# Moving gathered rows in 32-partition blocks and transposing them on VectorE in a top-2 expert layer

## Chip, cores and metric

The kernel runs on one core of a Trainium2 chip, in float32 throughout. The metric is device microseconds of one execution, as the median of several runs. Before the change the three runs gave 1540.99, 1541.81 and 1544.17 us, so the median is 1541.81 us.

## What is computed

The reference is a Mamba-2 block with a gated MLP, followed by a mixture of experts with eight experts of which each token takes two. `x` has 2048 rows (tokens) of 512 numbers.

```python
x = x + _L0_attn_ref(_layernorm(x), ...)      # Mamba-2 block and gated MLP
x = x + _L0_ffn_ref(_layernorm(x), Wr, Wg, Wu, Wd)

def _L0_ffn_ref(x, Wr, Wg, Wu, Wd):            # H=512, I=352, E=8, K=2
    probs = softmax(x @ Wr)                     # router, 8 columns
    topk_w, topk_idx = top_k(probs, 2); topk_w = topk_w / sum(topk_w)
    h = silu(x @ Wg[e]) * (x @ Wu[e])           # for the experts e of each token
    out = sum over the two e of  topk_w * (h @ Wd[e])
```

The change touches only the last part: how the rows of the normalised `x` get to the expert matmuls.

## The kernel before

**Stages.** Eight blocks of 256 tokens go through the Mamba part (`mamba`, `chunk`). From the third block on, the MLP of 512 tokens that are ready (`feed_forward`) is woven between them. The last MLP (tokens 1536 to 2047) runs alone. Then come the experts. The MLP leaves its result in DRAM (`out`), and the layer-normalised rows in `xnd` (all tokens) and `xnd1` (the first 1536): `route`, L586 to L673, writes them with `normed` (L594), transposes them for the router (`transposed`, L197), takes the two best experts per token, and scatters entries of token number and weight into per-expert lists in DRAM (L669, four indirect DMAs for each of two choices, issued by GpSimd).

**Tiles of the expert stage.** `table` (L932) turns the lists into tiles of 128 rows that all belong to one expert: ten from the first 1536 tokens (`NS1`, index `idx1`), 26 more once all tokens are routed (`idx2`). So 36 tiles (`NSA`) are always worked through, s = 0 to 35; three more stand behind a branch (L1123) that is taken only where they are filled. The weights of all eight experts lie in SBUF (`ew`).

**One tile** is this chain:

1. `gather(s)`, L1023: GpSimd issues an indirect DMA, 128 rows of 512 numbers from DRAM to `xg`, two buffers.
2. `front(s)`, L1031: four TensorE transposes of 128x128 into one PSUM bank (L201), and one ScalarE copy to SBUF (L203), which gives `xgT`: the 512 numbers of a row now lie on partitions.
3. `hidden(s)`, L1036: gate and up matmuls with `xgT` stationary (L1045, four steps of k, each for gate and up), in two halves with a pause between; SiLU on ScalarE (L1049), product on VectorE (L1050) gives `eh`.
4. `turned(s)`, L1053: three TensorE transposes of `eh`, copied out by VectorE (L1059, two thirds) and ScalarE (L1060, the last third) to `ehT`.
5. `back(s)`, L1063: three down matmuls (L1066; the last one reads ScalarE's third), scaling by the row's weight on VectorE (L1071), and an indirect DMA by GpSimd that adds the rows into `out` (L1072).

**Order.** TensorE's instructions stand as the program emits them (`manual_schedule`). For each tile s of `tiles()` (L1089) they are: transposes of tile s+1, first half of `hidden(s)`, transposes `turned(s-1)`, second half of `hidden(s)`, `back(s-1)`. The instructions of the other engines are put in order by a planner of the framework, which also inserts the waits. Each engine works its own queue strictly in order, and so a waiting instruction holds what stands behind it; a DMA issue stands in the queue of the engine that issues it. While tiles 0 to 4 run, the routing of the last 512 tokens is woven in (`second()`, L1112), and the second table comes out of it during tile 7.

**Buffers that matter.** `pmlp` has three buffers under the tag "mg", used by the MLP's weights (`mg`, `ms`, L526 and L539). `wk` has four under the tag "a" (the MLP's `a`, then `xgT` and `ehT`). `AHEAD = 2` (L1077) lets gathers be emitted two tiles ahead.

```python
    def transposed(src, dst, weight=None, kind="tr"):
        pt = bank(kind, [NK, P], "pt")
        for k in range(NK):
            nc.tensor.transpose(pt[:, k, :], src[:, k * P : (k + 1) * P], ident)
        if weight is None:
            nc.scalar.copy(dst, pt)
```

Of the kernel before, what the change touches and what calls it, by code (L numbers as in the profile page):

```python
# [9 lines left out]
F32 = mybir.dt.float32  # L10
I32 = mybir.dt.int32
AF = mybir.ActivationFunctionType
ALU = mybir.AluOpType
# [3 lines left out]
P = 128  # L17
T = 2048
D = 512
NK = D // P  # L20
# [12 lines left out]
FC = 128  # L33
NFC = DFF // FC
NE = 8
EI = 352
ET = [(0, 128), (128, 128), (256, 96)]


NS = (2 * T + NE * (P - 1)) // P  # L40

NS1 = 10


NSA = (2 * T + NE * (P // 2)) // P
EW = NK * 2 * EI + len(ET) * D
EPS = 1e-5
# [7 lines left out]
def mamba_mlp_moe(ctx, tc, x, w_in, w_out, w_gu, w_down, par, wr, wg, wu, wd, out):  # L55
# [3 lines left out]
    nc = tc.nc  # L59
# [13 lines left out]
    pmlp = ctx.enter_context(tc.tile_pool(name="pmlp", bufs=2, side="right"))  # L73
# [13 lines left out]
    w_o = pw.tile([P, 8, D], F32, name="w_o")  # L87
    wr_sb = const.tile([P, NK, NE], F32, name="wr_sb")

# [6 lines left out]
    def load_w_in(pair):  # L96
# [15 lines left out]
        out=tri, in_=ones, pattern=[[1, P]], compare_op=ALU.is_ge, fill=0.0, base=0, channel_multiplier=-1  # L112
# [3 lines left out]
        out=late, in_=ones, pattern=[[-1, P]], compare_op=ALU.is_gt, fill=0.0, base=0, channel_multiplier=1  # L116
# [3 lines left out]
    nc.gpsimd.memset(eps, EPS)  # L120
    rank = const.tile([P, NE], F32, name="rank")
    nc.gpsimd.iota(rank, pattern=[[-1, NE]], base=NE, channel_multiplier=0, allow_small_or_imprecise_dtypes=True)
    halo = pw.tile([P, 12, 3], F32, name="halo")
# [7 lines left out]
    upto = const.tile([P, NE, NE], F32, name="upto")  # L131
    nc.gpsimd.affine_select(
        out=upto, in_=ones[:, : NE * NE].rearrange("p (e f) -> p e f", e=NE), pattern=[[1, NE], [-1, NE]],
# [63 lines left out]
# [7 lines that stand above are left out]
        else:  # L204
            nc.vector.tensor_tensor(dst, pt, bc(weight, 2, P), ALU.mult)
# [121 lines left out]
    def finish(steps):  # L327
        while True:
            try:
                next(steps)  # L330
            except StopIteration as end:
                return end.value
# [187 lines left out]
    KH = NK // 2  # L520
# [65 lines left out]
    def route(fb, rows):  # L586

        mv2, rs2 = small("mv2", NJ, 2), small("rs2", NJ)
        for j in range(NJ):
            stats(small_p, rows[j], mv2[:, j, :])  # L590
        rsqrt_eps(rs2, mv2[:, :, 1])
        lg, l2, tmp = (small(n, NJ, NE) for n in ("lg", "l2", "tmp"))

        def normed(j):  # L594
            t = fb * NJ + j
            nc.scalar.dma_start(out=out[t * P : (t + 1) * P, :], in_=rows[j])
            xn = mid([D], f"xn{t}")
            nc.vector.tensor_scalar(xn, rows[j], mv2[:, j, 0:1], rs2[:, j : j + 1], ALU.subtract, ALU.mult)
            nc.scalar.dma_start(out=xnd[t * P : (t + 1) * P, :], in_=xn)
            if fb < NFB - 1:  # L600
                nc.scalar.dma_start(out=xnd1[t * P : (t + 1) * P, :], in_=xn)
            return xn

        def logits(j, xT):
            pl = bank("d", [NE], f"pl{fb}_{j}")
            for k in range(NK):
                nc.tensor.matmul(pl, xT[:, k, :], wr_sb[:, k, :], start=(k == 0), stop=(k == NK - 1))
            nc.vector.tensor_copy(lg[:, j, :], pl)

        xn = normed(0)  # L610
        yield
        for j in range(NJ):
            if j:
                logits(j - 1, xT)
            xT = mid([NK, P], f"xT{fb}_{j}")
            transposed(xn, xT)
            if j < NJ - 1:
                xn = normed(j + 1)
            yield
        logits(NJ - 1, xT)  # L620

        chosen = [small(n, NJ, NE) for n in ("o1", "o2")]
        m1, m2, *mr = (small(n, NJ) for n in ("rm1", "rm2", "mr1", "mr2"))

        def top(src, mx, mr, oh):

            nc.vector.tensor_reduce(mx, src, AX.X, ALU.max)
            nc.vector.tensor_tensor(tmp, src, bc(mx, 2, NE), ALU.is_equal)
            nc.vector.tensor_tensor(tmp, tmp, bc(rank, 1, NJ), ALU.mult)
            nc.vector.tensor_reduce(mr, tmp, AX.X, ALU.max)  # L630
            nc.vector.tensor_tensor(oh, tmp, bc(mr, 2, NE), ALU.is_equal)

        top(lg, m1, mr[0], chosen[0])
        nc.vector.scalar_tensor_tensor(l2, chosen[0], -3.0e38, lg, ALU.mult, ALU.add)
        top(l2, m2, mr[1], chosen[1])

        wt = [small(n, NJ) for n in ("wt1", "wt2")]
        nc.vector.tensor_tensor(m2, m2, m1, ALU.subtract)
        nc.scalar.activation(m2, m2, AF.Exp)
        nc.vector.tensor_scalar_add(wt[0], m2, 1.0)  # L640
        nc.vector.reciprocal(wt[0], wt[0])
        nc.vector.tensor_tensor(wt[1], m2, wt[0], ALU.mult)


        both, prior = small("both", NJ, NE), small("prior", NJ, NE)
        nc.vector.tensor_tensor(both, *chosen, ALU.add)
        nc.vector.tensor_copy(prior[:, 0, :], before)
        for j in range(1, NJ):
            nc.vector.tensor_tensor(prior[:, j, :], prior[:, j - 1, :], both[:, j - 1, :], ALU.add)
        nc.vector.tensor_tensor(before, prior[:, NJ - 1, :], both[:, NJ - 1, :], ALU.add)  # L650
        yield
        yield
        pr = bank("tr", [NJ, NE], f"pr{fb}")
        nc.tensor.matmul(pr, tri, both, start=True, stop=False)
        nc.tensor.matmul(pr, ones, prior, start=False, stop=True)
        nc.vector.tensor_copy(prior, pr)

        for n in range(2):

            at, to = small("at", NJ), small_p.tile([P, NJ], I32, name=f"to{n}", tag=f"to{n}")  # L660
            nc.vector.tensor_tensor(tmp, chosen[n], prior, ALU.mult)
            nc.vector.tensor_reduce(at, tmp, AX.X, ALU.add)
            nc.vector.scalar_tensor_tensor(at, mr[n], -float(T), at, ALU.mult, ALU.add)
            nc.vector.tensor_scalar_add(at, at, NE * T - 1.0)
            nc.vector.tensor_copy(to, at)
            entry = entries[:, n, fb * NJ : (fb + 1) * NJ, :]
            nc.vector.tensor_copy(entry[:, :, 1], wt[n])
            for j in range(NJ):
                nc.gpsimd.indirect_dma_start(  # L669
                    out=writers.pop(), out_offset=bass.IndirectOffsetOnAxis(ap=to[:, j : j + 1], axis=0),  # L670
                    in_=entry[:, j, :], in_offset=None,
                )
            yield  # L673
# [215 lines left out]
    for b in range(NB):  # L889
        fb, at = divmod(b, BPF)  # L890
# [132 lines left out]
    def gather(s):  # L1023
        n, (_, _, idx, _), src = of(s)
        xg = row(f"xg{s}")
        nc.gpsimd.indirect_dma_start(  # L1026
            out=xg, out_offset=None, in_=src, in_offset=bass.IndirectOffsetOnAxis(ap=idx[:, n : n + 1], axis=0)
        )
        return xg

    def front(s, xg):  # L1031
        xT = wk.tile([P, NK, P], F32, name=f"xgT{s}", tag="a", bufs=4)
        transposed(xg, xT)
        return xT

    def hidden(s, xT):  # L1036
        n, (exp_i, _, _, _), _ = of(s)
        e = nc.tensor.value_load(exp_i[0:1, n : n + 1], min_val=0, max_val=NE - 1)
        w = ew[:, bass.DynSlice(e, 1), :].rearrange("p a n -> p (a n)")
        pg = bank("g", [EI], f"epg{s}")  # L1040
        pu = bank("u", [EI], f"epu{s}")
        for k in range(NK):
            for a, ps in enumerate((pg, pu)):
                lo = (2 * k + a) * EI
                nc.tensor.matmul(ps, xT[:, k, :], w[:, lo : lo + EI], start=(k == 0), stop=(k == NK - 1))  # L1045
            if k == 1:
                yield
        h = mid([EI], f"eh{s}")
        nc.scalar.activation(h, pg, AF.Silu)  # L1049
        nc.vector.tensor_tensor(h, h, pu, ALU.mult)  # L1050
        return h, w
# [22 lines left out]
            compute_op=ALU.add,  # L1074
        )

    AHEAD = 2  # L1077
    rest = None
    got, xT = {}, {}

    def fetch(upto):

        for s in range(min(upto + AHEAD, NSA if rest else NS1)):
            if s not in got:
                got[s] = gather(s)
        if upto in got:
            xT[upto] = front(upto, got[upto])

    def tiles():  # L1089

# [32 lines left out]
    filled = nc.values_load(rest[0][0:1, NS - NS1 :], min_val=0, max_val=NS)  # L1123
    with tc.If(filled > NSA - NS1):
        for s in range(NSA, NS):
            h, w = finish(hidden(s, front(s, gather(s))))
            back(s, turned(s, h), w)


# [64 lines left out]
```

## Time and profile before

The profiled execution took 1540.27 us; its span from first to last instruction is 1538.6 us. Its granted TensorE clock is 0.994 of full speed.

| engine | busy us | share of span |
|---|---|---|
| TensorE matmuls (PE) | 1498.3 | 97% |
| TensorE weight loads (PEld) | 1021.0 | 66% |
| VectorE (DVE) | 749.8 | 49% |
| ScalarE (ACT) | 744.0 | 48% |
| GpSimd (POOL) | 425.5 | 28% |

The expert stage alone runs from about 1228 us to the end. In the stretch from 1300 to 1345 us the starts of one matmul group in successive tiles (the down matmuls at 1310.06, 1318.14, 1326.22, 1334.31) are 8.08 us apart: that is the period of one tile. From 1296 to 1400 us PE is busy in all of the 104.0 us, DVE in 22.1, ACT in 17.0 and POOL in 34.5; the DMA engines have a mean share of 0.40 there.

How to read a line of groups: source line, engine, operation, tile written and tiles read, size, and count; then busy time and the mean of one; then idle time of that engine just before, with what ended it. A busy PE isn't PE at its peak, since matmuls overlap: the pitch, from start to start, says more than the duration.

### The profile page before, as it was taken

The page shows a single profiled execution, that of the slowest core. Times are in us where ns is not written, and L with a number is a line of the kernel's source. Part 1 is how long each engine was busy: PE and PEld are TensorE (multiplying, and loading weights), DVE is VectorE, ACT ScalarE, POOL GpSimd, SP SyncE. Part 2 cuts the span into 40 slices and gives each one's busy share as a digit, 9 for nine tenths or more (in the row PEclk, how much of TensorE's full clock was granted, in tenths as well). Part 3 has the DMA queues.
Part 4 walks back from the last instruction along what each step waited for, and adds up shares of the span by engine and source line. Part 5 has one row for each costly group of instructions (what it writes and reads, how often), then busy time and mean ns, then how long its engine had stood idle before and what let it go on. Part 6 is the DMA issues. An engine that isn't in the chain of part 4 may idle for free. (4 is left out here: it accounts for less than half of the span.)

```text
span 1538.6 us, 18825 instructions
## 1 busy us (share of the span) xinstructions
PE 1498.3 (97%) x6153; PEld 1021.0 (66%) x6153; DVE 749.8 (49%) x1939; ACT 744.0 (48%) x1332; POOL 425.5 (28%) x537
## 2 busy tenths in 40 slices
PE   8899999999999999999999999999999999999996
PEld 7566577677667676767676677666776666566553
DVE  7776775645645564556454643334343433222221
ACT  5888967635663598458745754222221231111110
POOL 4432324424242212141212120411131124233321
PEclk9999999999999999999999999999999999999999
DMA  9444445545544554454335532426879434333332
GB/s 305 137 138 125 137 140 183 190 149 171 171 151 148 185 165 131 137 118 157 121 123 179 167 121 89 93 93 209 289 205 260 152 91 64 66 69 65 66 63 35
DMA packets 128241, 217.54 MB, mean 141 GB/s; under 512 B 12560, under 2 KB 72848, under 8 KB 128144
## 3 DMA queue, kind: packets, MB, share of 16 engines
q1 hardware_dynamic: 105376, 166.34, 35.6%
q0 software_dynamic: 9088, 18.91, 7.2%
q10 hardware_dynamic: 13680, 31.07, 5.4%
q8 instruction: 52, 0.85, 0.2%
q14 instruction: 45, 0.37, 0.1%
HBM read 175.48 MB, written 40.80 MB: 141 GB/s over the span
## 5 line engine op out<-in xcount | busy, mean ns | idle before, releaser
L691 PE MATMUL pd<-md,a 128*128 128x512 f32 x512 | 238.8, 593 | 0.8 <-DVE r L692 0.7
L340 PE MATMUL pm<-hT,wi 128*128 128x256 f32 x768 | 185.4, 386 | 3.7 <-DMA wi<-in_w_in 3.7
L340 PEld LDWEIGHTS pm<-hT,wi 128*128 128x128 f32 x768 | 141.7, 192 | 29.2 <-issue 7.9
L692 DVE TENSOR_TENSOR r<-r,pd 128x512 f32<-128x512 f32 x128 | 87.4, 684 | 150.6 <-PE pd L691 149.9
L691 PEld LDWEIGHTS pd<-md,a 128*128 128x128 f32 x512 | 96.9, 190 | 76.6 <-issue 65.8
L361 DVE SCALAR_TENSOR_TENSOR ca<-pre,params,ca 128x256 f32<-128x256 f32 x288 | 143.9, 557 | 0.3
L707 PE MATMUL py<-h2T,ms 128*128 128x256 f32 x512 | 131.7, 380 | 3.5 <-DMA ms<-late 2.6
L772 POOL TENSOR_TENSOR a<-a,up 128x256 f32<-128x256 f32 x64 | 47.0, 734 | 265.7 <-DVE up L766 225.8
L340 PE MATMUL pz<-hT,wi 128*128 128x256 f32 x512 | 117.0, 381 | 0.0
L490 PE MATMUL po<-w_o,zs 128*128 128x512 f32 x256 | 116.2, 607 | 0.0
L1045 PE MATMUL epg<-ew,xgT 128*128 x288 | 109.0, 460 | 0.2 <-ACT xgT L203 0.2
L1045 PE MATMUL epu<-ew,xgT 128*128 x288 | 108.7, 459 | 0.0
L707 PEld LDWEIGHTS py<-h2T,ms 128*128 128x128 f32 x512 | 95.4, 190 | 19.5 <-issue 2.3
L420 ACT ACT_TABLE_LOAD x75 | 96.2, 1283 | 21.5 <-DVE ncum L285 14.5
L340 PEld LDWEIGHTS pz<-hT,wi 128*128 128x128 f32 x512 | 94.8, 190 | 13.8 <-ACT zs L373 0.8
L1066 PE MATMUL epd<-ew,ehT 128*128 (+1 forms) x216 | 98.9, 593 | 1.0 <-DVE ehT L1059 1.0
L420 ACT ACTIVATE cum<-cum,ncum 128x128 f32<-128x128 f32 x256 | 85.7, 392 | 6.2 <-POOL cum L314 4.8
L490 PEld LDWEIGHTS po<-w_o,zs 128*128 128x128 f32 x256 | 49.5, 195 | 58.4 <-issue 57.3
L752 ACT COPY a<-px 128x256 f32<-128x256 f32 x64 | 23.6, 369 | 127.2 <-PE px L707 111.3
L1026 POOL DMA_INDIRECT xg<-xnd,idx x36 | 35.5, 985 | 154.4 <-PE pt L201 150.6
L422 DVE SCALAR_TENSOR_TENSOR cum<-cum,dt,psc 128x128 f32<-128x128 f32 x256 | 72.9, 339 | 5.8 <-PE psc L414 3.6
L203 ACT COPY xgT<-pt 128x512 f32<-128x512 f32 x36 | 21.0, 586 | 111.8 <-PE pt L201 111.8
(240 smaller groups left out, 2528.1 us busy)
## 6 DMA issues: line engine op xcount, KB each, us to landing
wi<-in_w_in SPq DMA_DIRECT2D x80, 512.0 KB, 3.8
ms<-late SPq DMA_DIRECT2D x48, 512.0 KB, 3.7
mg<-early SPq DMA_DIRECT2D x48, 384.0 KB, 3.8
md<-in_w_down SPq DMA_DIRECT2D x64, 256.0 KB, 4.0
cum<-rowsd SPq DMA_DIRECT2D x32, 512.0 KB, 4.1
late<-ms ACTq DMA_DIRECT2D x16, 512.0 KB, 2.7
ec<-rowsd SPq DMA_DIRECT2D x60, 128.0 KB, 3.4
xnd<-xn ACTq DMA_DIRECT2D x28, 256.0 KB, 3.8
```

What stands on the lines that cost most here:

```text
L340: nc.tensor.matmul(pm[:, m, :], w[:, k, m * P : (m + 1) * P], hT[:, k, :], start=(k == 0), stop=(k == NK - 1))
L361: nc.vector.scalar_tensor_tensor(ca, pre[:, m, k : k + TB], cw[:, k : k + 1], ca, ALU.mult, ALU.add)
L420: nc.scalar.activation(lt[:, half, i], lt[:, half, i], AF.Exp, bias=ncum[:, j, h : h + 1])
L422: nc.vector.scalar_tensor_tensor(lt[:, half, i], lt[:, half, i], dt[:, j, h : h + 1], psc[:, half, i], ALU.mult, ALU.mult)
L490: nc.tensor.matmul(po, y[:, m, :], w_o[:, m, :], start=(m == 0), stop=(m == 7))
L691: nc.tensor.matmul(pd, a[:, j * P : (j + 1) * P], d, start=(m == 0), stop=(m == 1))
L692: nc.vector.tensor_tensor(rows[j], rows[j], pd, ALU.add)
L707: nc.tensor.matmul(ps, w[:, k], m[:, k], start=(first and k == 0), stop=(k == KH - 1), skip_group_check=True)
L772: nc.gpsimd.tensor_tensor(a[:, 1], a[:, 1], up, ALU.mult)
L1026: nc.gpsimd.indirect_dma_start(out=xg, out_offset=None, in_=src, in_offset=bass.IndirectOffsetOnAxis(ap=idx[:, n : n + 1], axis=0))
L1045: nc.tensor.matmul(ps, xT[:, k, :], w[:, lo : lo + EI], start=(k == 0), stop=(k == NK - 1))
L1066: nc.tensor.matmul(pd, hT[:n, m, :], w[:n, NG + m * D : NG + (m + 1) * D], start=(m == 0), stop=(m == len(ET) - 1))
```

## The change

The normalised rows are written to DRAM with their 512 columns in another order: (q k c) in place of (k q c), with q = 4 blocks, k = 4 and c = 32. The router's weights `Wr` are permuted on the host to match. For the expert tiles, `transposed` is no longer called. In its place `moved` copies the gathered tile from SBUF to SBUF in sixteen DMAs of 32 partitions by 128 numbers (512 bytes a partition, 16 KB each), eight issued by SyncE (SP) and eight by ScalarE, so that block r of 32 rows and column block q land on partitions of block q. One VectorE instruction then transposes all 32x32 squares at once and writes `xgT`. `xq` takes one of the three "mg" buffers. Gathers are emitted three tiles ahead, moves for the tile at hand and the next.

```diff
+QD = 32
...
-            nc.vector.tensor_scalar(xn, rows[j], mv2[:, j, 0:1], rs2[:, j : j + 1], ALU.subtract, ALU.mult)
+            nc.vector.tensor_scalar(
+                xn.rearrange("p (q k c) -> p k q c", q=P // QD, k=NK),
+                rows[j].rearrange("p (k q c) -> p k q c", q=P // QD, k=NK),
+                mv2[:, j, 0:1], rs2[:, j : j + 1], ALU.subtract, ALU.mult,
+            )
...
-    def front(s, xg):
+    def moved(xg):
+        xq = pmlp.tile([P, NK, KH, FC], F32, name="xq", tag="mg", bufs=3)[:, :KH].rearrange("p a b f -> p (a b) f")
+        blocks = [slice(n * QD, (n + 1) * QD) for n in range(P // QD)]
+        for q, to in enumerate(blocks):
+            for r, of_ in enumerate(blocks):
+                (nc.scalar if r % 2 else nc.sync).dma_start(out=xq[to, r], in_=xg[of_, q * P : (q + 1) * P])
+        return xq
+
+    def front(s, xq):
         xT = wk.tile([P, NK, P], F32, name=f"xgT{s}", tag="a", bufs=4)
-        transposed(xg, xT)
+        nc.vector.transpose(
+            xT.rearrange("p k (r i) -> p r k i", i=QD), xq.rearrange("p r (k c) -> p r k c", k=NK)
+        )
         return xT
...
-    AHEAD = 2
+    AHEAD = 3
...
         for s in range(min(upto + AHEAD, NSA if rest else NS1)):
             if s not in got:
                 got[s] = gather(s)
+        for s in (upto, upto + 1):
+            if s in got and s not in at:
+                at[s] = moved(got[s])
         if upto in got:
-            xT[upto] = front(upto, got[upto])
+            xT[upto] = front(upto, at[upto])
...
-        "wr": a["Wr"],
+        "wr": a["Wr"].reshape(NK, P // QD, QD, NE).swapaxes(0, 1).reshape(D, NE),
```

More of the change, by code (lines that the diff above doesn't have):

```diff
@@ L1075, in back @@
         )
-    AHEAD = 2
+    AHEAD = 3
     rest = None
-    got, xT = {}, {}
+    got, at, xT = {}, {}, {}
     def fetch(upto):
@@ L1125, in mamba_mlp_moe @@
         for s in range(NSA, NS):
-            h, w = finish(hidden(s, front(s, gather(s))))
+            h, w = finish(hidden(s, front(s, moved(gather(s)))))
             back(s, turned(s, h), w)
```

## The prediction, made before the run

> **What bounds the kernel now.** I read the table of busy times, then the groups by line for the expert stage, then the timeline of single tiles there. TensorE is busy for 97% of the span, and the change takes work from TensorE in the expert stage alone. There it never waits:
>
> ```profile
> L1045 PE MATMUL epg<-ew,xgT 128*128 x288 | 109.0, 460 | 0.2 <-ACT xgT L203 0.2
> L201 PE MATMUL pt<-ident,xg 128*128 128x128 f32 x144 | 21.6, 273 | 0.0
> ```
>
> The first is the gate matmul, with 0.2 us of idle time in 36 tiles; the second is what goes. Its 21.6 us busy overlap with neighbours, so I take the pitch from the timeline of one tile (start, duration, engine, line):
>
> ```profile
> 1318.14 2.74 PE L1066 MATMUL epd<-ew,ehT 128*128 x6
> ...
> 1320.72 0.60 PE L201 MATMUL pt<-ident,xg 128*128 128x128 f32 x4
> ...
> 1321.16 0.76 PE L1045 MATMUL epg<-ew,xgT 128*128 x2
> ```
>
> Down matmuls to transposes 2.58 us, transposes to gate 0.44 us. Near the end, where no tile is left to transpose, the gate follows the down matmuls directly, so nothing else is hidden in the 0.44:
>
> ```profile
> 1512.12 2.74 PE L1066 MATMUL epd<-ew,ehT 128*128 x6
> ...
> 1514.69 0.76 PE L1045 MATMUL epg<-ew,xgT 128*128 x2
> ```
>
> A tile is then 8.08 us: down 2.58, transposes 0.44, half of hidden 2.37, turned 0.33, half of hidden 2.37.
>
> **What goes.** 36 x 0.44 = 15.8 us of TensorE, and the 0.24 us in which the first tile waited for ScalarE's copy: 16.0 us. ScalarE loses 36 copies of 0.58 us, VectorE gains 36 transposes; neither bounds (17.0 and 22.1 of 104 us busy between 1296 and 1400).
>
> **VectorE's transpose** has no row. Nearest are whole passes over 128x512 f32: 0.55 us (L598), 0.69 (L692), 0.75 (L1071). The Trainium skill, "VectorE: DVE Perf Modes", section "The three transpose paths", gives VectorE 311 ns for 128x128 bf16, 32x32 blocks only, and its rules send a 128x128 transpose to TensorE. Four times 311 ns would be 1.24 us. I take 0.7 and keep 0.55 to 1.24. In the built order it stands between the copy to `ehT` and the product `eh`, which TensorE needs some 5 us after hidden ends (down 2.58, half of hidden 2.37), so either price is covered.
>
> **The moves, price of one.** Nearest is the 16 KB store of 32 rows by 512 bytes in the Mamba part (min/median/max in ns, then landing in us):
>
> ```profile
> L278 SPq DMA_DIRECT2D rowsd<-rows x8: 317/330/1642, 21.0 to 821.5; - x8
> ...
> DMA to landing us min/median/max: 1.4/2.6/9.4
> ```
>
> and of the store that follows it:
>
> ```profile
> L279 SPq DMA_DIRECT2D rowsd<-rows_e x8: 373/452/454, 26.3 to 823.6; - x8
> ...
> DMA to landing us min/median/max: 1.4/3.5/10.6
> ```
>
> So an issue costs 0.33 us alone and 0.45 close behind another, and landing takes 1.4 us in quiet and 2.6 or 3.5 between half-megabyte loads. The expert stage has no such loads; the 256 KB stores of L596 land there in 2.0 us. I take 0.45 and 1.8, and keep 1.4 to 3.5.
>
> A rule speaks against this edit. "DMA: Bandwidth & Descriptors", section "Anatomy of one DMA", fits about 2.0 us fixed plus bytes/436e3 to a DMA issued by GpSimd, and its rules for kernel authors want small transfers coalesced. If the fixed part were paid one after the other, eight per queue would be 16.3 us a tile against a period of 7.64, or 36 x 8.7 = 310 us more. The trace says that they overlap: four 128 KB loads of L324 were issued within 2.51 us (30.65 to 33.16), faster than one lands (3.4). But not without limit: in the built order every hardware-queue DMA waits on one of eight semaphores, so it waits for the DMA that used it last, about eight earlier. A tile's sixteen therefore go in two rounds: 4 issues per engine, 1.7 us; the second round no sooner than one landing; 1.7 us more. From the rows' arrival to ScalarE's last issue: about 3.7 us.
>
> **Steady tiles.** ScalarE's queue per tile holds SiLU (0.46), the `ehT` copy (0.26) and 8 issues (3.6): 4.3 of 7.64 us, and with the landing between the rounds (2 us at most) still below it. In the built order the moves run up to five tiles ahead of their use, bounded by three `xq` buffers; rows and moves arrive over a tile early. SP is free. 512 packets of 512 bytes a tile, at no more than the mean 83 ns of the hardware queue (35.6% x 16 x 1538.6 us / 105376 packets), are 2.7 us on 16 engines: share 0.35 beside today's 0.40. Cost of a steady tile: nothing, and 7.64 us apart. If that cover went, ScalarE would be the bound.
>
> **Where the queue does hold TensorE.** Moves of tile s wait for gather s, and what stands behind them on ScalarE waits too. Three places:
>
> *Start.* Gather 0 is issued at 1210.62, behind `idx`, and lands 3.5 us later, at 1214.1. In the built order ScalarE has one move before the copy of `up` (1213.27 before) and seven before the copy of px of MLP step 15 (1215.79 before). Issues at 1214.2, 1214.65, 1215.1, 1215.55, then the second round at 1216.0 and 1216.45; the copy at 1216.95 instead of 1215.79. TensorE's next product, due 1216.45, starts at 1217.4: **+1.1**. Later VectorE waits for `xq` before row additions that free PSUM; with 1.8 us landing these fall in slack.
>
> *The routing's scatter.* Tile 9 of the first table is gathered, in the built order of GpSimd, behind the eight list scatters. Before, tile 8 stood there:
>
> ```profile
> 1265.67 1.58 POOL L1072 DMA_INDIRECT out<-ey,idx  x1 [0.30 <-DVE at L662]
> 1267.56 0.99 POOL L669 DMA_INDIRECT lists<-entries,to  x1 [0.30 <-DVE ehT L1059]
> ...
> 1276.61 0.96 POOL L669 DMA_INDIRECT lists<-entries,to  x1 [0.30 <-issue]
> 1277.87 0.98 POOL L1026 DMA_INDIRECT xg<-xnd,idx  x1 [0.30 <-issue]
> ```
>
> That gather landed in 7.8 us where others take 3.3, since the scatters' packets were ahead of it: 18.1 us from the first scatter to landed rows. ScalarE's eight moves of tile 9 stand ahead of the `ehT` copy of tile 4. First scatter at 1264.7 (TensorE is 1.4 us ahead by then, and a gather that stood before it is gone), rows at 1282.8, eight issues to 1286.5, copy to 1286.8. TensorE reaches that third of tile 4 at 1276.7 (hidden 5 ends at 1277.27 less 2.25 won, plus two of three down matmuls, 1.72). **+10.1**. This is the largest cost, and the late thing after it is nothing: SP's load of `rows` is behind the same moves but needed only after hidden 7.
>
> *The clock after it.* A gap of 3.71 us early in the kernel was followed by this:
>
> ```profile
> 26.75 3.40 PE L340 MATMUL pm<-hT,wi 128*128 128x256 f32 x15
> 29.99 0.38 PE L387 MATMUL ptx<-ident,xb 128*128 128x128 f32 x2
> 34.08 5.38 PE L340 MATMUL pm<-hT,wi 128*128 128x256 f32 x16 [3.71 <-DMA wi<-in_w_in]
> ```
>
> 16 matmuls in 5.38 us, against 16/15 x 3.40 = 3.63; the granted clock was 0.54 and 0.61 in 34 to 38 us. **+1.8**.
>
> *Second table.* Gather 10 can start 1.5 us after hidden 7 and lands 3.4 to 4.4 later; its moves stand before the `ehT` copy of tile 7, ready at 8.8 to 9.8 us. TensorE needs it at 9.75 (index matmul 0.38, down 2.58, hidden 5.07, 1.72). **0 to 0.5**; I take 0.3.
>
> The strided write of `xn` passes over the same 512 numbers: 0.55 us as before, hidden behind TensorE.
>
> Sum: -16.0 + 1.1 + 10.1 + 1.8 + 0.3 = **-2.7 us**, from 1540.27 to 1537.6. The median of the runs shown is 1.5 us above that execution, so **1539.2 us**. A difference under 0.2%, 3.1 us, can't be told from none here.
>
> **Rivals.**
>
> *Slow landings (slower).* If 16 KB land in 3.5 us, as the second row has it, the second rounds come late everywhere. Start: ScalarE's copy slips to 1218.6 (+2.2), and VectorE's waits for `xq` 1, `xq` 2 and then the routing's statistics come out of their slack, some 5 more. At tile 4 +1.7 (11.8), at the second table 0.7, then 1.5 and 2 in the two tiles that follow. -16.0 + 7 + 11.8 + 1.8 + 4.2 = +8.8: **1550.6**. It decides from about 2.6 us on, where the start costs some 4.5. For it: both medians. Against: the quiet minimum and L596.
>
> *ScalarE isn't held at tile 4 (faster).* If tile 9's rows arrive like other tiles' (3.3 us), the 10.1 and 1.8 shrink to about 1: -16 + 1.1 + 1 + 0.3: **1528**. Against: the 7.8.
>
> *Moves become the period (much slower).* If a move cost 0.9 us to issue, as when both queues' issues take turns, ScalarE needs 8 x 0.9 + 0.7 = 7.9 us plus part of a landing, say 9.5 a tile: 36 x 1.4 = 50 more than before: **1592**. Against: 0.45.
>
> *Not done at all:* the built order has no transposes of `xg` left on TensorE, so that falls away.
>
> **Chances.** Forecast 0.50 (own range 1534 to 1544), slow landings 0.33, not held 0.12, moves as the period 0.05. Range **1529 to 1553**. Faster: 0.22 of the forecast's and the 0.12, 0.34. Same: 0.23 of the forecast's and a little of slow landings, 0.26. Slower: the rest, 0.40.
>
> **What will tell.** Period 7.64 us late in the stage; one TensorE gap of some 10 us in `epd` of tile 4 ended by ScalarE's `ehT`; the landing of `xq` (1.8 or above 2.6); the start of the first gate matmul (about 1228.8, before 1228.90). Wrong if the period isn't 7.64, or no gap stands at tile 4.

## The result and the profile after

| kernel | median us | lowest to highest | runs |
|---|---|---|---|
| before | 1542.18 | 1540.99 to 1544.17 | 4 |
| after | 1564.44 | 1562.96 to 1567.22 | 4 |

The ratio is 1.0145, with a 95% interval of 1.0127 to 1.0163: 22 us slower, outside the range of 1529 to 1553, on the side of the two slower rivals and beyond the one that was priced at 1550.6.

The profiled execution of the changed kernel took 1567.22 us, 2.8 above its median, and the one before 1.9 below its own. So I compare one stage, from the index matmul of the first table (L986 after, L980 before) to the end: 1208.24 to 1538.6 before, 1213.83 to 1565.4 after. That is **330.4 and 351.6 us: 21.2 more**, about the difference of the medians.

First the groups of the page. L1084, L1063 and L1078 were L1066, L1045 and L1060; the first line is the one of before, the rest are of after.

```profile
L1066 PE MATMUL epd<-ew,ehT 128*128 (+1 forms) x216 | 98.9, 593 | 1.0 <-DVE ehT L1059 1.0
L1084 PE MATMUL epd<-ew,ehT 128*128 (+1 forms) x216 | 102.0, 603 | 20.6 <-issue 10.3
L1063 PE MATMUL epg<-ew,xgT 128*128 x288 | 113.0, 475 | 0.3 <-issue 0.3
L1078 ACT COPY ehT<-pht 96x128 f32<-96x128 f32 x36 | 9.4, 262 | 209.2 <-DMA xq<-xg 104.9
```

The gate matmuls still hardly wait (0.3 us): `xgT` is in time. The down matmuls wait 20.6 us where they had waited 1.0, and the copy they need stood 104.9 us behind moves. The timeline of TensorE, cut to the matmuls that waited, shows where (start, duration, and in brackets the idle time before it):

```profile
1224.07 1.13 PE L713 MATMUL px<-h2T,ms 128*128 128x256 f32 x4 [1.86 <-ACT a L765]
1234.39 1.98 PE L697 MATMUL pd<-md,a 128*128 128x512 f32 x4 [0.60 <-DVE xgT L1049]
1245.16 1.08 PE L202 MATMUL pt<-ident,xn 128*128 128x128 f32 x4 [4.06 <-DVE xn L600]
1291.45 2.08 PE L1084 MATMUL epd<-ew,ehT 96*128 x2 [7.82 <-issue]
1303.55 1.13 PE L1084 MATMUL epd<-ew,ehT 96*128 x2 [2.03 <-ACT ehT L1078]
1328.90 1.13 PE L1084 MATMUL epd<-ew,ehT 96*128 x2 [1.69 <-ACT ehT L1078]
1339.26 1.59 PE L1084 MATMUL epd<-ew,ehT 96*128 x2 [2.45 <-issue]
1351.16 1.12 PE L1084 MATMUL epd<-ew,ehT 96*128 x2 [2.31 <-ACT ehT L1078]
1362.38 1.12 PE L1084 MATMUL epd<-ew,ehT 96*128 x2 [3.31 <-ACT ehT L1078]
```

"Issue" on the 7.82 is a wait for several semaphores; the copy `ehT` that came last ran from 1291.14, so it is ScalarE's too. From tile 3 on (1291), all these gaps are in the last third of the down matmuls, the third that ScalarE copies. After 1372 there is none but the last tiles' own, and the period is what was forecast, 7.64 us:

```profile
1431.73 2.74 PE L1084 MATMUL epd<-ew,ehT 128*128 x6
1439.37 2.74 PE L1084 MATMUL epd<-ew,ehT 128*128 x6
```

Behind the longer gaps TensorE ran slowly. Three stretches (span, length, busy time and count of PE, PEld, DVE, ACT, POOL, then the granted clock, DMA share, GB/s):

```profile
1245.00:1254.00 9.00, 8.84 (x27) 5.77 (x28) 1.58 (x5) 2.95 (x5) 0.96 (x1) 0.66 0.46 142
1291.00:1298.00 7.00, 6.55 (x18) 4.02 (x19) 4.31 (x17) 0.73 (x2) 1.62 (x1) 0.68 0.58 59
1336.00:1345.00 9.00, 6.55 (x17) 3.37 (x16) 2.09 (x4) 0.73 (x2) 2.07 (x3) 0.81 0.34 77
```

The trace's record of the clock gives half speed in four stretches of this part of the stage: 1244.21 to 1251.04, 1288.58 to 1295.41, 1339.78 to 1343.20 and 1363.68 to 1367.09. Half of the time in which TensorE was busy there is the loss to the clock; what lies inside a gap is idle time already. The account of the stage (the last gap of the second table, 0.32 us at 1363.83, is counted too):

| place | idle us | slow clock us | sum | forecast |
|---|---|---|---|---|
| start, 1206 to 1254 | 6.5 | 2.9 | 9.5 | 1.1 |
| routing, 1254 to 1312 | 9.9 | 2.0 | 11.8 | 11.9 |
| second table, 1312 to 1372 | 10.1 | 3.3 | 13.4 | 0.3 |
| transposes gone | | | -16.0 | -16.0 |
| together | | | 18.7 | -2.7 |

Measured: 21.2. Part of the missing 2.5 us is that a gap costs more than its idle time: down matmuls that are cut in two are busy for 1.88 and 1.13 us at full clock, uncut for 2.74. At 0.27 us for each of the six gaps of that kind, I estimate 1.6; the rest stays open. The question for the experiments is why ScalarE's copy came late at three places, two of which had been priced at next to nothing.

The longest gap, 7.82 us, is one of late landings. `ACTq` and `SPq` are DMA issues; L1032 is a gather (the first is tile 8's, the second tile 9's) and L675 the first list scatter:

```profile
1276.40 0.99 POOL L1032 DMA_INDIRECT xg<-xnd,idx  x1 [4.24 <-DMA xq<-xg]
1279.58 1.00 POOL L675 DMA_INDIRECT lists<-entries,to  x1 [0.30 <-DVE at L670]
...
1283.74 0.51 SPq L1044 DMA_DIRECT2D xq<-xg  x1
...
1289.74 0.99 POOL L1032 DMA_INDIRECT xg<-xnd,idx  x1 [0.31 <-issue]
1290.53 0.51 ACTq L1044 DMA_DIRECT2D xq<-xg  x1
1291.14 0.26 ACT L1078 COPY ehT<-pht 96x128 f32<-96x128 f32 x1 [15.09 <-issue]
```

Tile 8's rows came in time: SP issued its first move of them at 1279.97, 3.6 us after the gather. ScalarE's move of 1290.53, the last ahead of the copy, waits in the trace for the semaphore of SP's move of 1283.74. So that 16 KB move, issued among the scatters, took over 6 us to land.

The queue of ScalarE behind the second table shows something else. x8 is eight issues in the time given:

```profile
1322.34 6.15 ACTq L1044 DMA_DIRECT2D xq<-xg  x8
1328.58 0.26 ACT L1078 COPY ehT<-pht 96x128 f32<-96x128 f32 x1 [11.29 <-DMA xq<-xg]
...
1329.25 9.60 ACTq L1044 DMA_DIRECT2D xq<-xg  x12
1338.94 0.26 ACT L1078 COPY ehT<-pht 96x128 f32<-96x128 f32 x1 [9.73 <-DMA xq<-xg]
...
1340.20 10.55 ACTq L1044 DMA_DIRECT2D xq<-xg  x12
1350.85 0.26 ACT L1078 COPY ehT<-pht 96x128 f32<-96x128 f32 x1 [10.21 <-DMA xq<-xg]
```

Eight issues took 6.15 us from the arrival of the rows (the forecast had 3.7), and then twelve and twelve stood between two copies, where a steady tile has eight. The planner places moves several tiles early; as long as rows are late, ScalarE must work off that lead before it gets to copies that TensorE needs now. I call this the theory of the lead. A count bears it out here: at the copy of tile 7 (1328.58) the moves of tile 10 had been issued, at that of tile 10 (1362.07) those of tile 15. That is 40 issues in 33.5 us, two tiles' worth more than three tiles need, and three periods of 7.64 are 22.9.

### The profile page after: what moved, and what is told of

Its sections match the earlier page's. It is cut to its first block, busy times and chain, and to the rows that moved or that the text cites. A ratio compares the mean times of both kernels' runs of the same rounds, so it can differ in the third digit from the quotient of the medians.

```text
span 1565.4 us, 19436 instructions
## 1 busy us (share of the span) xinstructions
PE 1496.4 (96%) x6009; PEld 1013.1 (65%) x6009; DVE 771.6 (49%) x1975; ACT 723.1 (46%) x1296; POOL 425.2 (27%) x537
## 5 line engine op out<-in xcount | busy, mean ns | idle before, releaser
L341 PE MATMUL pm<-hT,wi 128*128 128x256 f32 x768 | 188.7, 391 | 3.1 <-DMA wi<-in_w_in 3.1
L362 DVE SCALAR_TENSOR_TENSOR ca<-pre,params,ca 128x256 f32<-128x256 f32 x288 | 140.6, 545 | 0.3
L1084 PE MATMUL epd<-ew,ehT 128*128 (+1 forms) x216 | 102.0, 603 | 20.6 <-issue 10.3
L491 PE MATMUL po<-w_o,zs 128*128 128x512 f32 x256 | 113.0, 593 | 3.1 <-POOL w_o L819 3.1
L1063 PE MATMUL epg<-ew,xgT 128*128 x288 | 113.0, 475 | 0.3 <-issue 0.3
L1063 PE MATMUL epu<-ew,xgT 128*128 x288 | 111.4, 469 | 0.0
L1078 ACT COPY ehT<-pht 96x128 f32<-96x128 f32 x36 | 9.4, 262 | 209.2 <-DMA xq<-xg 104.9
L421 ACT ACT_TABLE_LOAD x75 | 96.2, 1283 | 21.2 <-DVE ncum L286 14.1
L1090 POOL DMA_INDIRECT out<-ey,idx x36 | 57.1, 1587 | 113.8 <-DVE ey L1089 94.1
L1084 PEld LDWEIGHTS epd<-ew,ehT 128*128 128x128 f32 (+1 forms) x216 | 40.4, 191 | 64.2 <-issue 43.0
```

The lines of the kernel that those rows point to most:

```text
L341: nc.tensor.matmul(pm[:, m, :], w[:, k, m * P : (m + 1) * P], hT[:, k, :], start=(k == 0), stop=(k == NK - 1))
L362: nc.vector.scalar_tensor_tensor(ca, pre[:, m, k : k + TB], cw[:, k : k + 1], ca, ALU.mult, ALU.add)
L421: nc.scalar.activation(lt[:, half, i], lt[:, half, i], AF.Exp, bias=ncum[:, j, h : h + 1])
L491: nc.tensor.matmul(po, y[:, m, :], w_o[:, m, :], start=(m == 0), stop=(m == 7))
L1084: nc.tensor.matmul(pd, hT[:n, m, :], w[:n, NG + m * D : NG + (m + 1) * D], start=(m == 0), stop=(m == len(ET) - 1))
L1090: nc.gpsimd.indirect_dma_start(out=out, out_offset=bass.IndirectOffsetOnAxis(ap=idx[:, n : n + 1], axis=0), in_=y, in_offset=None, compute ...
```

## Experiments

All ratios are to the kernel before on the same chip, whose medians there lay between 1543.85 and 1550.23 us; below 1 is faster. The stage is that of the one profiled execution; before it is 330.4, after 351.6.

| run | ratio | 95% interval | stage us |
|---|---|---|---|
| e1 new column order, no moves | 0.9986 | 0.9971 to 1.0001 | 330.3 |
| e2 SP's eight moves alone | 0.9909 | 0.9888 to 0.9929 | 321.6 |
| e3 sixteen on SP | 1.0559 | 1.0544 to 1.0574 | 418.4 |
| e4 moves behind the copy of u-3 | 1.0254 | 1.0212 to 1.0297 | 362.9 |
| e5 ScalarE's eight moves alone | 1.0083 | 1.0065 to 1.0101 | 345.0 |
| e6 moves from tile 13 | 0.9992 | 0.9978 to 1.0005 | 333.4 |
| e7 no moves for tiles 8, 9 | 1.0102 | 1.0077 to 1.0126 | 345.5 |
| e8 twelve moves | 1.0347 | 1.0301 to 1.0393 | 386.9 |
| e9 second table paced | 1.0402 | 1.0381 to 1.0423 | 390.8 |
| e10 moves from tile 10 | 1.0034 | 1.0015 to 1.0052 | 333.3 |
| e11 all paced | 1.0563 | 1.0528 to 1.0598 | 419.7 |
| e12 moves and transposes paced | 1.0435 | 1.0415 to 1.0456 | 400.4 |
| e13 every other tile, SP | 1.0108 | 1.0090 to 1.0126 | 344.3 |
| e14 three row buffers | 1.0179 | 1.0160 to 1.0198 | 361.0 |
| e15 e13 with own row buffers | 0.9996 | 0.9983 to 1.0010 | 325.9 |
| e16 two thirds, the same | 1.0002 | 0.9990 to 1.0014 | 325.8 |
| **e17 every other tile, 128-byte pieces** | **0.9967** | 0.9954 to 0.9979 | 325.7 |
| e18 two thirds, the same | 0.9974 | 0.9961 to 0.9988 | 329.1 |

### e1: is it the new column order?

```diff
-            at[s] = moved(got[s])
+            at[s] = got[s]          # front(): TensorE transposes, ScalarE copies
```

> The xn columns are written in the new order and wr is permuted, but every tile is transposed by TensorE as before, gathers two ahead and no moves; it takes plain blocks of 128 columns, so the output mixes columns. Queue theory (moves stand in ScalarE's in-order queue ahead of work that TensorE needs): the strided write costs nothing, 1542 +- 2, and the first index matmul of table 1 at about 1208 to 1210 as before. Rival, the strided write or the new columns cost the 5.6 us by which that matmul came later in the changed kernel: 1547 to 1548.

Nothing: 0.9986, and a stage of 330.3 us beside 330.4. The 5.6 us by which the changed kernel's profile reached the index matmul later were that execution's, not the edit's: e1 reached it at 1207.17, and e2, which is the changed kernel up to there, at 1206.15.

### e2 and e5: the same moves, in one queue or the other

```diff
-                (nc.scalar if r % 2 else nc.sync).dma_start(out=xq[to, r], ...)
+                if r % 2 == 0:      # e5: if r % 2, and nc.scalar
+                    nc.sync.dma_start(out=xq[to, r], ...)
```

> Only SP's eight moves of a tile are made; ScalarE issues none, VectorE transposes the moved half twice, so half of the rows are wrong. Queue theory: no ehT wait is left, 1542 - 16 + 0 to 3 = 1526 to 1529. Rival, the rows simply arrive late (slow gathers behind the list scatters, slow landings): TensorE then waits for xgT instead, at tiles 8 to 11, and the time stays above 1540.

> The mirror of the run with SP's moves alone: only ScalarE's eight moves of a tile are made, SP issues none, VectorE transposes the moved half twice (half of the rows are wrong). Same number of DMAs, bytes and landings as there. Queue theory: the moves still stand ahead of the ehT copies, so TensorE waits for ehT at the routing and behind the second table, 12 to 25 us in all: 1538 to 1552. Rival, the number of moves and their eight semaphores decide, not the queue: as with SP's half, 1529 +- 3.

This pair decides. Both make eight moves of 16 KB a tile; only the issuing engine differs. TensorE's waits for ScalarE's `ehT` (total us, times, longest), first in SP's half and then in ScalarE's:

```profile
PE epd L1086 <- ACT ehT L1080: 0.9, 1, 0.9
```

```profile
PE epd L1086 <- ACT ehT L1080: 12.8, 4, 8.6
```

SP's half is 14 us faster than the kernel before, ScalarE's half 13 us slower, each beside the kernel before on its own chip. The number of DMAs and their bytes are the same, so those 27 us come from where the moves are issued. Landings aren't quite alike: by the trace's semaphore updates from 1400 to 1500 us, a move landed 1.8 us after its issue in the median of e2 and 2.4 in that of e5. But late landings alone don't cost TensorE anything: in e2 a tile's moves among the list scatters took up to 8.2 us (issued at 1277.29, landed at 1285.46), and TensorE had no wait there.

### e3: then all of them on SP?

```diff
-                (nc.scalar if r % 2 else nc.sync).dma_start(
+                nc.sync.dma_start(
```

> All sixteen moves of a tile on SP. Queue theory: no ehT copy waits for a move; what decides is SP's issue pitch. At 0.45 us (the prediction's) 7.2 us a tile, under the period of 7.64: about 1530. At 0.51 to 0.60 us, as the changed kernel's issues took, 8.2 to 9.6 us a tile: SP becomes the period, 36 x 0.5 to 2.0 us more than 1527: 1545 to 1597, TensorE waiting for xgT. Rival, landings or rows are late whatever the queue: as the changed kernel, 1560 or more, with gaps at the same three places only.

The gaps at special places don't stand out any more; every tile is late. The down matmuls start 10.3 us apart:

```profile
1391.01 2.85 PE L1084 MATMUL epd<-ew,ehT 128*128 x6 [2.24 <-DVE ehT L1077]
1401.29 2.85 PE L1084 MATMUL epd<-ew,ehT 128*128 x6 [2.38 <-DVE ehT L1077]
```

SP issued 20 moves in 12.66 us, 0.63 each, and sixteen of these are 10.1 us. A single queue has room for eight, not for sixteen. With 0.45 us it would have had room.

### e7, e6, e10: where does it cost?

```diff
+    def by_blocks(s):
+        return s not in (NS1 - 2, NS1 - 1)   # e6: s >= NS1 + 3; e10: s >= NS1
...
-            at[s] = moved(got[s])
+            at[s] = moved(got[s]) if by_blocks(s) else got[s]
```

> As the changed kernel, but tiles 8 and 9, whose rows and moves fall among the list scatters, are transposed by TensorE (in plain blocks, so their rows are wrong). Queue theory: the 7.8 and 2.0 us gaps in epd and the slow clock behind them go (13 us), 0.9 us of transposes come back: 1564 - 12 = 1552. Rival, any tile's moves that fall there hold the queue, since the landings of all DMAs are late then: the gap moves to another tile and the time stays at 1560 or more.

> Tiles 0 to 12 are transposed by TensorE (in plain blocks of 128 of the reordered columns, so their rows are wrong), tiles 13 to 35 by moves and VectorE; gathers two ahead in the first table, three in the second. Queue theory: the three places that hold TensorE have no move near them, 23 x 0.44 = 10.1 us are won: 1532 to 1535 against 1542 to 1544. Rival, the moves cost in any tile (contention, or a held queue in the steady part too): 1540 or more.

> Moves from tile 10 on as the planner places them; tiles 0 to 9 by TensorE in plain blocks of the reordered columns (their rows are wrong). The control of the paced kernel. Theory of the lead: 11.4 us are won and 8 to 12 given back at tiles 7 to 11: within 4 us of the kernel before, gaps in epd ended by ScalarE's ehT. Rival, the second table's late gathers alone make the gaps: the paced kernel has them too, and both come out alike.

e7 is 15.7 us slower than before where 10 had been forecast from the theory of the queue, and the changed kernel 22. The gaps of 7.8 and 2.0 us went; one of 5.59 came at 1295, this time ended by VectorE's `ehT`, so about half of the win moved on. e6 missed its forecast of 1532 to 1535: it is where the kernel before is, though no table or routing is near its first move. It lost the 10 us again where its moves begin: TensorE waited 2.83 us at 1349 and 3.54 at 1362 for `ehT`, with a slow clock after it; in the 24 us from 1338.2 to 1362.2 ScalarE issued 29 moves, three and a half tiles' worth, and got to one copy in between. So it isn't the second table that costs but the beginning of moves, as the lead would have it:

```profile
1340.74 8.19 ACTq L1044 DMA_DIRECT2D xq<-xg  x12
1349.03 0.26 ACT L1087 COPY ehT<-pht 96x128 f32<-96x128 f32 x1 [9.05 <-DMA xq<-xg]
...
1351.43 10.64 ACTq L1044 DMA_DIRECT2D xq<-xg  x13
1362.17 0.26 ACT L1087 COPY ehT<-pht 96x128 f32<-96x128 f32 x1 [11.19 <-DMA xq<-xg]
```

e10 begins at tile 10 and behaves alike, with two waits for `ehT` of 8.0 us together; at 5 us above the kernel before it is a little beyond its forecast.

### e4, e9, e11, e12, e8: taking the lead away by hand

If the lead is what costs, moves placed later should help. `issue_after` puts what is emitted behind a given instruction in its engine's queue. In short:

```diff
+            with tc.issue_after(copied[s - 3]):   # ScalarE's copy to ehT of tile s-3
+                at[s] = moved(got[s])             # e9, e11, e12: three of ScalarE's eight here,
+            with tc.issue_after(gated[s - 2]):    # and five behind the SiLU of tile s-2
...
+                    with tc.issue_after(turned_v[s - 2]):   # e12: VectorE's copy to ehT
+                        xT[s] = front(s, at[s])
```

> The changed kernel, with the moves of tile u issued only behind the ehT copy of tile u-3 in ScalarE's queue instead of up to five tiles early. Queue theory: the gaps in epd at tiles 3, 4 and 7 to 10 go (13 + 12 us with their clock), and most of the start's 4.1 us: 1564 - 25 to 34 = 1530 to 1539; the eight issues now stand between ehT and the next SiLU, 6 us in a slack of about 6.5, so small waits on eh may show. Rival, slow landings: the gaps move to xgT and the time stays above 1555.

> Correct and meant to be faster than both: tiles 0 to 9 (first table) are gathered from rows in the old order and transposed by TensorE; rows for the second table are stored in the new order by a second pass of VectorE, and its 26 tiles go by moves, paced by hand: three of ScalarE's moves of tile u behind the ehT copy of tile u-3, five behind the SiLU of tile u-2, never earlier. Theory of the lead (the planner puts moves up to five tiles early, and ScalarE has to work off that lead while ehT copies wait, some 8 to 12 us wherever moves begin): without the lead it costs 0 to 2 us, and 26 x 0.44 = 11.4 us are won: 9 to 11 us below the kernel before. Rival, moves at two to three tiles' distance come too late: TensorE waits for xgT or for VectorE's ehT behind it, no gain or slower, as in the run with twelve moves.

> The changed kernel with all tiles from 3 on paced as in the paced kernel (three moves behind ehT of u-3, five behind SiLU of u-2). Theory of the lead: the second table's 12 us and the steady waits on eh of the run with all eight behind the copy go; what stays is the start (about 10) and the routing (about 11, since moves issued among the list scatters land late): 1542 - 16 + 21 + 2 = about 1549, between before and the changed kernel. Rival, the lead is nothing and lateness of rows decides: 1560 or more.

> The paced second table, and VectorE's transpose of tile u placed behind its own ehT copy of tile u-2 as well, so that no ehT copy stands behind a move or a transpose on either engine. If only the place in the two queues decides: 26 x 0.44 = 11.4 us won, 0 to 3 given back at the start of the second table: 8 to 11 us below the kernel before. If the moves themselves are too slow for this distance (from rows to landed moves about 8 us of a period of 7.64, with gathers waiting for them): TensorE waits for xgT in each tile, 10 us or more above the kernel before.

> The four diagonal blocks of a tile are copied by VectorE on their own partitions, twelve are moved: ten on SP, two on ScalarE, those of tile u behind the ehT copy of tile u-3. Queue theory: SP needs 10 x 0.63 = 6.3 us of a period of 7.64, ScalarE is held for 1.3 us where it has slack: 1542 - 16 + 2 to 6 = 1528 to 1533, faster than both kernels. Rival, VectorE takes over the holding (its transposes and copies wait for moves and rows ahead of its ehT copies and of the routing): 1540 or more, with TensorE waiting for VectorE's ehT.

All five were slower than the changed kernel, and far from what the theory forecast; the rivals named beforehand for e8, e9 and e11, moves that come too late and VectorE holding its `ehT`, came true. Each time the wait took another place. In e4 eight issues stood ahead of SiLU, and the tiles took 8.2 to 9.0 us:

```profile
1402.15 5.61 ACTq L1044 DMA_DIRECT2D xq<-xg  x8
1407.80 0.46 ACT L1067 ACTIVATE eh<-epg 128x352 f32<-128x352 f32 x1 [5.63 <-DMA xq<-xg]
```

In e9 (and in e11 and e8, where TensorE waited 67 and 49 us for VectorE's `ehT`) VectorE's transpose now stood ahead of VectorE's own copy to `ehT`, and waited for moves that came just in time or later:

```profile
1450.96 0.71 DVE L1061 STREAM_TRANSPOSE xgT<-xq 128x512 f32<-128x512 f32 x1 [6.31 <-DMA xq<-xg]
1451.60 0.39 DVE L1089 COPY ehT<-pht 128x256 f32<-128x256 f32 x1
```

In e12 the transpose was moved away too, and ScalarE stood again:

```profile
1440.31 8.84 ACTq L1047 DMA_DIRECT2D xq<-xg  x5
1449.25 0.26 ACT L1090 COPY ehT<-pht 96x128 f32<-96x128 f32 x1 [8.49 <-DMA xq<-xg]
```

Five issues took 8.84 us, and e12's trace shows why: ScalarE's third of them, at 1447.35, waits for a semaphore whose last user is SP's first move of the next tile (1443.85), which waits for that tile's gather, which waits for a row buffer. The moves of both queues take the same eight semaphores in turn, so spacing one queue by hand ties it to the other's future. My theory of the lead was right about where the loss falls, and wrong that less lead is the cure: with two row buffers and shared semaphores, moves that begin later are just late. No run took the lead away and left the rest as it was, so the lead's own price is argued from the queues and the counts, not isolated.

### e14: is it the gathers' wait for a row buffer?

```diff
-        xg = row(f"xg{s}")
+        both[s] = pmlp.tile([P, NK, KH, FC], F32, name="xq", tag="mg", bufs=3)
+        xg = both[s][:, KH:].rearrange("p a b f -> p (a b) f")
```

> The changed kernel with the gathered rows in the free half of the buffers of xq, so that three tiles of rows are held instead of two; moves, queues and transposes as they were. If gathers waiting for moves make most of the second table's loss (about 12 us) and part of the routing's: 8 to 14 us below the changed kernel, ratio to before 1.006 to 1.009. If ScalarE's eight issues ahead of its ehT copies make it, whenever rows come: within 5 us of the changed kernel, ratio 1.011 to 1.018.

Not as this edit does it: with three row buffers the kernel is no faster (28 us over before; its interval touches the changed kernel's), and small waits for `ehT`, 0.15 to 1.3 us, now also stand in the steady part. But rows and `xq` now share a buffer, and gathers wait for VectorE's transpose instead (27.6 us in 19 waits between 1300 and 1540). So that more row buffers alone wouldn't help isn't shown.

### e13, e15, e16: nothing in ScalarE's queue

```diff
+        return s >= NS1 and s % 2 == 1        # e16: s % 3 != 1
...
-                (nc.scalar if r % 2 else nc.sync).dma_start(
+                nc.sync.dma_start(
```

The other tiles read a second copy of the rows in the old order and are transposed by TensorE. e15 and e16 have e14's row buffers too.

> Only every other tile of the second table (13 tiles) goes by moves, all sixteen on SP, which at 0.63 us needs 10.1 of 15.7 us for them; the others are gathered from a copy of the rows in the old order and transposed by TensorE; nothing of it in ScalarE's queue. Theory of the queue: 13 x 0.44 = 5.7 us below the kernel before, no gap ended by ehT. Rival, VectorE's transposes hold its ehT copies as in the paced run: gaps ended by VectorE's ehT, no gain.

> As the run with every other tile of the second table on SP alone, and the moved tiles' rows have buffers of their own. There a pair of tiles took 17.1 us: a gather, 3.4 us to land, sixteen moves of 0.63, and the next gather waited for them. Without that wait SP needs 10.1 us of a pair's 15.7: 13 x 0.44 = 5.7 us below the kernel before, ratio 0.995 to 0.998. Rival: VectorE's transpose still stands ahead of the work that TensorE needs and waits for its moves: slower than before, with gaps ended by VectorE's eh or ehT.

> The same with two of three tiles of the second table moved (17 tiles): SP needs 20.3 us of 23.4. Theory: 17 x 0.44 = 7.5 us below the kernel before, ratio 0.994 to 0.997. Rival: SP comes too late for VectorE, as in the run with all moves on SP: 10 us or more above it.

e13 shows the gathers' wait alone, with no ScalarE in it: a pair of tiles took some 17 us, and TensorE waited 13.9 us for VectorE's product `eh`, which stood behind a transpose. With own row buffers (e15) every wait but the ends is gone and the stage is 4.5 us shorter, but the kernel isn't faster. By these two numbers, what the stage won is lost ahead of it.

### e17, e18: the version that is faster than both

Here the rows stay in the old order, so nothing ahead of the expert stage is touched. A move takes four pieces of 128 bytes from each row:

```diff
+                nc.sync.dma_start(
+                    out=xq[to, r].rearrange("p (k c) -> p k c", k=NK),
+                    in_=xg[of_].rearrange("p (k q c) -> p k q c", q=P // QD, k=NK)[:, :, q],
+                )
```

> The kernel before, except that every other tile of the second table (13 tiles) is moved by SP, with row buffers of its own and rows in the old order: each move takes four pieces of 128 bytes from each of 32 rows, 2048 packets a tile instead of 512. If pieces of 128 bytes cost no more to issue: 13 x 0.44 = 5.7 us below the kernel before, ratio 0.9955 to 0.998, nothing lost ahead of the expert stage. If they take so much longer to issue or land that VectorE waits for xq: slower than before.

> The same with two of three tiles (17 tiles): SP needs 20.3 of 23.4 us if a move still takes 0.63 us to issue: 7.5 us below the kernel before, ratio 0.994 to 0.997. If a move of pieces takes 0.75 us or more, SP becomes the bound: above the kernel before.

e17 is 0.33% faster than the kernel before (0.21 to 0.46), 5 us where 5.7 had been forecast. Its tiles take 7.64 and 8.08 us in turn, with no wait in this stretch:

```profile
1433.08 2.74 PE L1098 MATMUL epd<-ew,ehT 128*128 x6
1440.72 2.74 PE L1098 MATMUL epd<-ew,ehT 128*128 x6
1448.80 2.74 PE L1098 MATMUL epd<-ew,ehT 128*128 x6
```

Four pieces cost hardly more to issue than one (median 0.600 us, in e15 0.589). e18 won less than its count promised: TensorE waited 2.56 us at 1334 and 0.91 at 1323 for `eh`, in the first tiles that are moved. Since e15 and e17 have the same stage (325.9 and 325.7 us) and differ by 0.29%, I estimate the price of the second copy of the rows at some 4 us. With the two intervals it could be 2 to 7, the two ran on different chips, and the profiles can't show it: e17's reached the stage at 1220.16, e15's at 1216.00, though e17 changes nothing ahead. Whether VectorE's second pass or the third store costs it wasn't tried.

## Why the prediction was wrong

- **What goes, 16.0 us.** Right. The period late in the stage is 7.64 us, and SP's half of the moves alone came to 14 below the kernel before.
- **VectorE's transpose, 0.7 us.** Right: 0.71.
- **The strided write, nothing.** Right (e1).
- **Price of a move.** "I take 0.45 and 1.8." The issue was mis-sized: its median was 0.60 us, and 0.70 to 0.75 from start to start where both queues issue, waits for semaphores included (two in 1.41 us, six in 4.47), so that a tile's eight took 5.2 to 6.6 us of ScalarE where 3.6 had been entered. A nearer row stood in the prediction itself: four loads of L324 issued in 2.51 us are 0.63 each. (They landed in 4.8 us or more, not in the 3.4 given for them.) The landing was too low as well: by the trace's semaphore updates, some 2.8 us in the median from 1400 to 1500 us, where it cost nothing, and over 6 among the list scatters.
- **Steady tiles cost nothing.** Right after 1372. But the reason given, "the moves run up to five tiles ahead of their use [...]; rows and moves arrive over a tile early", is the step that failed elsewhere. It takes the lead as given and enters its building at nothing. While the lead is being built, at the start, behind the routing and behind the second table, the same order makes ScalarE issue up to a tile and a half of moves between two copies.
- **Start, +1.1.** The first step was there (1.86 instead of 1.1). The sentence after it, "with 1.8 us landing these fall in slack", was wrong: ScalarE's table load for the rows' statistics stood 14.5 us behind moves of later tiles, and TensorE waited 4.06 us for `xn`.
- **The routing's scatter, +10.1.** The size came out (9.9 idle), but by luck. The forecast cause was rows held up behind the scatters. That was tile 9's gather, which landed 7.3 us after its issue (7.8 forecast) and cost 2.0 us. The other 7.8 came from tile 8, whose rows were in time: ScalarE's queue held the copy of tile 3 because a move landed late, which had been priced at 1.8 us.
- **The clock, +1.8.** Right behind the one gap it was priced for (2.0), but four gaps were followed by a slow clock: 8.3 in all.
- **Second table, 0.3.** The largest miss. Only tile 10's moves had been counted ahead of one copy, with 3.7 us from rows to last issue; it took 6.2, and then twelve and twelve followed. 13.4 us.
- **The rivals.** Slow landings pointed the right way, and landings were slow; they had a part in the gap of 7.8 us. But they aren't what makes the loss: e2 has them, up to 8.2 us, and not the loss. "The moves become the period" didn't come about with two queues, but its 0.9 was nearer to the 0.70 to 0.75 from issue to issue than 0.45, and with one queue (e3) it came true.

## What to carry to other kernels

A small DMA was paid here in the queue of the engine that issued it, so give it to one that has nothing TensorE needs, and count the issues: here an engine had room for eight in 7.64 us, not for sixteen. When a planner places such issues several units early, price the places where that lead must be built (the beginning, and after any late input), not just the steady state; if you then space them by hand, look first at which buffers and semaphores tie them to the next unit. It paid to move only as much as the free queue takes, and to leave the stages ahead alone.

## What the hardware showed that I hadn't expected

- Issuing a 16 KB move between SBUF partitions cost its engine 0.51 us at the least and 0.59 to 0.60 in the median, while stores of the same shape to DRAM in the Mamba part took 0.33 to 0.45; packets of 128 bytes in place of 512 hardly changed it (0.585 and 0.600).
- The clock fell to half after short gaps, and which ones depended on when they came. The half-speed stretches start at 1244.21, 1288.58, 1339.78 and 1363.68: 13, 15 and 7 times 3.413 us apart. In the 3.41 us before 1339.78 TensorE was idle for 2.45 us. The gap of 2.31 us before 1351.16, after which the clock was 1.00, is cut in two by a point of the same grid, 1350.02. Summed window by window of this grid over the twenty traces, from 1205 us to 1525, TensorE at full clock was idle for 2.0 us or more in 59 windows, and half speed followed each time; it followed 11 of the 1706 windows with less. The Trainium skill, "TensorE: Matmul & The Clock Gate", section "Part 1: The HAM clock gate", gives an idle window of some 3.4 us as what it takes. The length agrees with the grid, but 2.0 us of idle time in it were enough here, and the measurement stands.
- Moves issued while GpSimd's list scatters were under way took much longer to land than the 1.8 us (median) of e2's steady tiles: up to 8.2 us in e2, and 7.6 in e4 (issued at 1288.87, landed at 1296.49, VectorE's transpose at 1296.67).
